# A hybrid scan and expert kernel on one core: a fuller plan for the experts beside the scans, and another order in the last stage

## The chip, the core and the metric

The kernel runs on one core of a Trainium2 chip. A core has a matrix engine (TensorE, PE in the profile; PEld are its weight loads), VectorE (DVE), ScalarE (ACT), GpSimd (POOL) and SyncE (SP), which here only issues DMAs. Each engine works through its own instructions in the order in which they stand; semaphores make it wait for others. The metric is the device time in microseconds, the median of the runs shown.

## What is computed

Two images of 256 channels and 4096 positions go through two layers. Layer 0 is a selective scan (a state-space model with 16 states per channel) with a residual. Layer 1 is a pair of such scans with 512 inner channels, one forward, one backward over the positions, with a residual, and then a mixture of eight small networks ("experts"):

```python
x = x + scan(group_norm(x))                       # layer 0, 256 inner channels
t = tokens(x)
n = layer_norm(layer_norm(t))
t = t + layer_norm(t) + scan_f(n) + flip(scan_b(flip(n)))   # layer 1, 512 inner channels each
n = layer_norm(t)
w = softmax(mean(n, over the two images) @ Wr + br)          # one weight per position and expert
h = relu(bn(n @ W1[e] + b1[e]))                              # for each of the 8 experts e
h = relu(bn(h @ W2[e] + b2[e]))
t = t + sum_e w[e] * (h @ Wo[e] + bo[e])
```

The routing weights `w` need both images. The experts' networks up to `h @ Wo[e]` need only one image's `n`, so they can run before `w` is known.

## The kernel before

Everything is float32. Positions are cut into 8 chunks of T = 512; a chunk of one image is held as two tiles of 128 channels. There are six scan jobs one after another: for each image layer 0, layer 1 forward, layer 1 backward. A job takes its 8 chunks in order.

**The scans and their slots.** The work beside the scans is laid out in slots: slot `2*g + h` is half `h` of quad `g`, and there are 640 quads, so 1280 slots. In each slot the emitting loop puts, in this order: DMA issues on SP, loads that have become due, TensorE's work (`pe`, then the sums over states `emit_sum`, then `pe2`), ScalarE's work (the carry, the next slot's decays L664, then `act`), VectorE's scan L690 and gates, the products with C (L699 on VectorE, L715 on GpSimd) and GpSimd's products L654. `sl.put(slot, queue, fn)` hangs any other work into a slot of a queue. The quads' buffer `bq` has six copies; TensorE's sums L723 free them.

**Features.** When a chunk of the backward job is done, `features` computes its layer-norm for the experts: mean on TensorE, centre on VectorE (L794), squares on ScalarE (`fsq`, L799), variance on TensorE (`fvar`, L804), root on ScalarE, division on VectorE (L809), and a store to DRAM (`nf_dram`, L814), each in a slot of its own, counted from the slot in which the chunk is stored. `ready` lists from which slot on the chunk may be used. The last chunk of image 1 has no slots left and gets its norm in the last stage.

**Experts beside the scans.** A pair is one expert on one chunk of one image; there are 2 x 8 x 8 = 128. A pair's three layers are 12 products of 128x512 (each layer: two output halves of two products). The planner `experts` walks over the slots and keeps two running sums: how many products TensorE is behind (a slot has room for `PE_ROOM` = 3.8 of them, and no half layer is added where more than `PE_BEHIND` would be behind) and the same for ScalarE. It also looks whether one of three PSUM banks is free. `follows` says from which slot a half layer may come: two slots after its input, and a number of slots after the last use of the weights' single buffer by the pair before (the `5` below; 6 for a chunk's first product), because `load_w` (L932) loads the weights three slots after that use. `emit_experts` then hangs the products (L912), activations (L923) and stores of the unweighted output `u` into their slots. Seventy-four pairs are placed so: all of image 0 (64), chunk 7 of image 1 (8) and two pairs of chunk 6.

**The last stage.** What the planner did not place runs after the scans, from L1062 on. `whole` are the chunks both of whose images are done (chunk 7), `rest` the others from the highest down (6, 5, ... 0). All experts' weights stay in SBUF; those not needed first are loaded in the first pairs (`weights`). For a chunk `i`, `load_n` (L1086, on GpSimd's DMA queue) brings both images' `n` into a tile with six buffers, `both` (L1108, GpSimd) adds them, `logits` (L1115) and `spread` (L1140 to 1146) make the routing weights and broadcast them through DRAM into `wb`, `bias` (L1163, L1166) adds the output biases, and `add_early` (L1170 to 1172) loads an early pair's `u`, multiplies it by its weight and adds it on VectorE. These steps are spread over the pairs of `rest` as `side` work. A pair computes two layers (L1201, L1205), `weigh` (L1212, VectorE) multiplies the hidden tile by the routing weight one pair later, and `last_layer` (L1220) multiplies by Wo another pair later. That is, the list `waiting` holds two pairs.

Of the kernel before, what the change touches and what calls it, by code (L numbers as in the profile page):

```python
# [42 lines left out]
F32 = mybir.dt.float32  # L43
# [4 lines left out]
P = 128  # L48
NB, C, L = 2, 256, 4096
KC = C // P  # L50
T = 512
# [28 lines left out]
E = 8  # L80


PE_ROOM, PE_BEHIND = 3.8, 2.5
ACT_ROOM, ACT_BEHIND = 2.6, 1.2
V_CW, V_CB, V_DB, V_D, V_A = 0, 4, 5, 6, 7
NV = V_A + NS
# [45 lines left out]
def hybrid_kernel(ctx: ExitStack, tc: tile.TileContext, a: dict, out: bass.AP):  # L132
# [45 lines left out]
    def rsqrt(dst, src, eps, scale=1.0):  # L178
        nc.scalar.activation(dst, src, AF.Ln, bias=eps, scale=scale)
        nc.scalar.activation(dst, dst, AF.Exp, scale=-0.5)  # L180
# [5 lines left out]
    with ExitStack() as st:  # L186
# [594 lines left out]
        def features(b, c, v, s0):  # L781

            featured.add((b, c))

            def mean():
                v["ps"] = psp.tile([P, T], F32, tag="ps", name=f"fmean_{b}{c}")
                for k in range(KC):
                    nc.tensor.matmul(
                        v["ps"], mean_w, v["x"][:, k, :], start=(k == 0), stop=(k == KC - 1)
                    )  # L790

            def centre():
                v["cen"] = wk.tile([P, KC, T], F32, tag="cen", name=f"fcen_{b}{c}")
                nc.vector.tensor_tensor(v["cen"], v["x"], over_channels(v["ps"]), ALU.subtract)  # L794

            def square():
                for k in range(KC):
                    v["sq", k] = wk.tile([P, T], F32, tag="th", name=f"fsq_{b}{c}{k}", bufs=3)
                    nc.scalar.activation(v["sq", k], v["cen"][:, k, :], AF.Square)  # L799

            def variance():
                v["var"] = psp.tile([P, T], F32, tag="ps", name=f"fvar_{b}{c}")
                for k in range(KC):
                    nc.tensor.matmul(  # L804
                        v["var"], mean_w, v["sq", k], start=(k == 0), stop=(k == KC - 1)
                    )

            def divide():
                nc.vector.tensor_tensor(v["cen"], v["cen"], over_channels(v["var"]), ALU.mult)  # L809

            for d, queue, fn in (
                (0, "pe", mean), (1, "dve", centre), (2, "act", square), (3, "pe", variance),
                (4, "act", lambda: rsqrt(v["var"], v["var"], eps5)), (5, "dve", divide),
                (6, "sp", lambda: nc.sync.dma_start(nf_dram[b][:, c, :, :], v["cen"])),  # L814
            ):
                sl.put(s0 + d, queue, fn)
            sl.count(s0, 2, 0, (1,))
            sl.count(s0 + 1, 0, 2)
            sl.count(s0 + 3, 2, 2, (2,))
            ready.append((s0 + 8, b, c))  # L820

        def scales():

# [23 lines left out]
        def experts():  # L847

            last = 2 * nq - 6
            banks = sorted(sl.banks, key=lambda r: r[0])  # L850

            def fits(slot):

                at = sum(b[0] <= slot for b in banks)
                both = banks[:at] + [(slot, slot + 1, 0)] + banks[at:]
                return all(
                    both[k - 3][1] + both[k][2] <= both[k][0] for k in range(max(3, at - 2), min(len(both), at + 4))
                    if at in range(k - 3, k + 1)
                )

            def sums_in(slot):
                n, h = divmod(slot % 16, 2)
                return 1.25 * len(SUMS.get((n, h), ())) + (1 if (n, h) in ((2, 0), (6, 0)) else 0)

            todo = [(at, b, c, e) for at, b, c in sorted(ready) for e in range(E)]
            behind = act_behind = 0.0
            times = [[], [], []]

            def follows(l):

                k, m = divmod(len(times[l]), KC)
                if k == len(todo):
                    return None
                waits = [(l - 1, k * KC + 1, 2)] if l else []
                if m:
                    waits.append((l, k * KC, 0))
                elif k:

                    waits.append((l, k * KC - 1, 6 if l == 0 and todo[k][-1] == 0 else 5))
                    if l < 2:  # L880
                        waits.append((l + 1, k * KC - 1, 0))
                if any(n >= len(times[w]) for w, n, _ in waits):
                    return None
                return max([todo[k][0] + 3] + [times[w][n] + d for w, n, d in waits])

            for slot in range(last):
                behind = max(0.0, behind) + sl.products.get(slot, 0) + sums_in(slot) - PE_ROOM
                act_behind = max(0.0, act_behind) + sl.acts.get(slot + 1, 0) - ACT_ROOM
                for l in (2, 1, 1, 0, 0):
                    at = follows(l)  # L890
                    if at is None or slot < at:
                        continue
                    if behind + 2 > PE_BEHIND or act_behind + 1.3 > ACT_BEHIND or not fits(slot):
                        break
                    banks.insert(sum(b[0] <= slot for b in banks), (slot, slot + 1, 0))
                    times[l].append(slot)
                    behind += 2
                    act_behind += 1 if l == 2 else 1.3
            put = [
                (*item[1:], [times[l][k * KC + m] for l in range(3) for m in range(KC)])  # L900
                for k, item in enumerate(todo) if (k + 1) * KC <= len(times[2])
            ]
            emit_experts(put)
# [158 lines left out]
    with ExitStack() as st:  # L1062
# [12 lines left out]
        for i in range(NCH - 1, -1, -1):  # L1075
            (whole if all(first[b, i] == E for b in range(NB)) else rest).append(i)

        def load_n(i):

            for b in range(NB):  # L1080
                n[b, i] = mk.tile([P, KC, T], F32, tag="n", name=f"n_{i}{b}", bufs=6)
                if (b, i) in featured:
                    src = nf_dram[b][:, i, :, :]
                else:
                    src = t_dram[b][:, :, i * T : (i + 1) * T]
                nc.gpsimd.dma_start(n[b, i], src)  # L1086
# [107 lines left out]
            nc.sync.dma_start(we[name, e], a[name][e].rearrange("(k p) n -> p k n", p=P))  # L1194

        def layer(x, l, e, tag):
            h = mk.tile([P, KC, T], F32, tag=f"h{l}", name=f"h{l}_{tag}", bufs=2 + l)
            for m in range(KC):
                ps = psp.tile([P, T], F32, tag="ps", name=f"hp{l}_{tag}_{m}")
                for k in range(KC):  # L1200
# [10 lines left out]
        def weigh(b, i, e, h):  # L1211
            nc.vector.tensor_tensor(h, h, over_channels(wb[i][:, e, :]), ALU.mult)  # L1212
# [39 lines left out]
        nc.sync.dma_start(bo, a["bo"])  # L1252
        layer_norm(rest[0])
        both(rest[0])
        weights = [("Wo", order[0])]
        for k in range(2, E):
            weights += [("W1", order[k]), ("W2", order[k]), ("Wo", order[k - 1])]
# [5 lines left out]
        for at, (b, i, e) in enumerate(pairs):  # L1263
# [6 lines left out]
                logits(i)  # L1270
            elif at == 1:
                spread(i)
            if waiting:
                weigh(*waiting[-1])
            waiting.append((b, i, e, h))
            if len(waiting) > 2:
                last_layer(*waiting.pop(0))
            done[i] += 1
            work = side[i] if at > 1 else []
# [111 lines left out]
```

## Time and profile before

The three runs took 5184.88 us in the median (5181.89 to 5185.45).

| what | value |
|---|---|
| the profiled execution's own time | 5183.55 us |
| its span on the core | 5181.8 us |
| mean granted TensorE clock | 0.917 |
| last product with the state sums (L723) | 4501.9 us |
| first product of the last stage (L1201) | 4527.3 us |
| pairs in the last stage | 54 |
| DMA over the span | 160 GB/s |

The page gives busy times over the whole span; since the kernel has a long stage with scans and a short one without, the stretches of the span are to be read one by one. A slot's pace can be read from VectorE's gates (L742), of which one falls on every eight slots: 54.5 us for sixteen slots in the steady parts.

### The profile page before, as it was taken

What the parts mean: (1) busy time and instruction counts of PE and PEld (TensorE: products, weight loads), DVE (VectorE), ACT (ScalarE), POOL (GpSimd) and SP (SyncE); (2) the same over time, 40 slices, a digit from 0 to 9 for tenths busy, and PEclk for the clock granted to TensorE, in tenths of its full rate; (3) what the DMA queues carried; (4) which work ended last, traced back from release to release, by engine and by line L of the source; (5) the groups of instructions that cost most, each with busy time, mean ns of one, the idle gap of its engine ahead of it and who ended that gap; (6) DMA issues with size and microseconds to landing.
All of it is one profiled execution on the core that took longest, in us unless ns stands there. A gap on an engine that the chain in (4) does not pass through costs nothing. (4 is left out here: it accounts for less than half of the span.)

```text
span 5181.8 us, 47299 instructions
## 1 busy us (share of the span) xinstructions
PE 4292.9 (83%) x14920; PEld 1483.9 (29%) x14920; DVE 4577.8 (88%) x3083; ACT 3681.3 (71%) x7462; POOL 4410.4 (85%) x1438
## 2 busy tenths in 40 slices
PE   5677677766668898888888888889899899689999
PEld 1222122222122233332222233223333333234444
DVE  6998999999999999999989999999999999746333
ACT  5778677777767888888887788888788888522332
POOL 5998999999999999999989999999999999611010
PEclk8888888887889999999999999999999999889999
DMA  4454433344334554555555544455544555354322
GB/s 176 154 178 163 154 127 139 129 152 154 135 131 160 195 185 164 182 171 196 191 185 177 191 159 174 155 181 191 178 165 165 173 183 175 117 189 155 111 104 77
DMA packets 314731, 834.47 MB, mean 161 GB/s; under 512 B 35240, under 2 KB 102064, under 8 KB 272496
## 3 DMA queue, kind: packets, MB, share of 16 engines
q1 hardware_dynamic: 310768, 806.15, 45.1%
q0 software_dynamic: 3712, 25.30, 1.3%
q8 instruction: 118, 1.93, 0.1%
q14 instruction: 133, 1.09, 0.1%
HBM read 647.18 MB, written 184.16 MB: 160 GB/s over the span
## 5 line engine op out<-in xcount | busy, mean ns | idle before, releaser
L654 POOL TENSOR_TENSOR bq<-rxdt,bc 128x2048 f32<-128x2048 f32 x640 | 2893.3, 4543 | 26.9 <-issue 11.8
L664 ACT ACTIVATE da<-rdt,w_a 128x512 f32<-128x512 f32 x2560 | 1756.5, 686 | 98.4 <-DVE bq L690 53.0
L690 DVE TENSOR_TENSOR_SCAN da<-da,h_state,bq 128x1024 f32<-128x1024 f32 x664 | 1559.2, 2348 | 63.8 <-ACT da L664 34.4
L715 POOL TENSOR_TENSOR bq<-bq,bc 128x2048 f32<-128x2048 f32 (+1 forms) x280 | 1180.0, 4214 | 22.5
L690 DVE TENSOR_TENSOR_SCAN bq<-da,h_state,bq 128x1024 f32<-128x1024 f32 x456 | 1058.6, 2338 | 20.3 <-ACT da L664 20.2
L723 PE MATMUL y<-bq,stack 128*32 128x512 f32 x5120 | 765.4, 691 | 347.4 <-POOL bq L715 324.1
L699 DVE TENSOR_TENSOR bq<-da,bc 128x1024 f32<-128x1024 f32 x760 | 926.5, 1219 | 15.9
L912 PE MATMUL e<-eh,ew 128*128 128x512 f32 x1184 | 578.6, 619 | 59.1 <-ACT eh L923 16.9
L709 ACT COPY h_state<-da 128x2 f32<-128x2 f32 x759 | 119.5, 157 | 680.0 <-DVE bq L699 678.5
L675 ACT ACTIVATE bq<-h_state,bq,a 128x1 f32<-128x1 f32 x1120 | 430.0, 384 | 0.7 <-POOL bq L654 0.2
L1205 ACT ACTIVATE h<-hp,of,sc 128x512 f32<-128x512 f32 x216 | 167.9, 778 | 347.4 <-PE hp L1201 330.3
L723 PEld LDWEIGHTS y<-bq,stack 128*32 128x32 f32 x5120 | 144.0, 118 | 906.1 <-POOL bq L715 461.1
L452 PE MATMUL conv<-xs,w_conv 64*64 64x512 f32 x2560 | 329.8, 604 | 24.4 <-ACT xs L436 21.4
L414 PE MATMUL z<-nx,w_in 128*128 128x512 f32 x640 | 324.7, 640 | 25.0 <-DVE sp L513 12.4
L414 PE MATMUL xs<-nx,w_in 128*128 128x512 f32 x640 | 317.5, 626 | 28.2 <-DVE xc L466 13.3
L912 PEld LDWEIGHTS e<-eh,ew 128*128 128x128 f32 x1184 | 214.2, 193 | 419.0 <-issue 209.0
L912 PE MATMUL e<-en,ew 128*128 128x512 f32 x592 | 286.1, 616 | 43.1 <-DVE sz L543 15.9
L761 PE MATMUL o<-sz,w_out 128*128 128x512 f32 x640 | 304.6, 616 | 0.0
L730 PE MATMUL y<-xc,w_d 128*128 128x512 f32 x320 | 193.6, 689 | 66.0 <-DVE sz L742 55.4
L517 POOL TENSOR_TENSOR xdt<-sp,xc 128x512 f32<-128x512 f32 x160 | 203.5, 1275 | 51.8 <-DVE sp L513 51.8
L923 ACT ACTIVATE eh<-e,of,sc 128x512 f32<-128x512 f32 x296 | 224.3, 770 | 30.5 <-PE e L912 29.9
L501 PE MATMUL dt<-dbc,w_dt 64*128 64x512 f32 x320 | 192.2, 695 | 41.2 <-ACT dbc L488 27.0
(138 smaller groups left out, 5045.5 us busy)
## 6 DMA issues: line engine op xcount, KB each, us to landing
rxdt<-xdtd SPq DMA_DIRECT2D x160, 1024.0 KB, 6.5
rdt<-dtd SPq DMA_DIRECT2D x160, 1024.0 KB, 6.3
bc<-bcd SPq DMA_DIRECT2D x384, 256.0 KB, 3.2
dtd<-sp SPq DMA_DIRECT2D x160, 256.0 KB, 3.6
xdtd<-xdt SPq DMA_DIRECT2D x160, 256.0 KB, 3.4
ew<-in_W SPq DMA_DIRECT2D x148, 256.0 KB, 4.9
u<-eu SPq DMA_DIRECT2D x74, 512.0 KB, 4.0
u<-u SPq DMA_DIRECT2D x74, 512.0 KB, 4.0
```

Source lines behind the costliest of these rows:

```text
L414: nc.tensor.matmul(ps, job.w["in", half][:, k, j * P : (j + 1) * P], rhs, start=(k == 0), stop=(k == KC - 1),)
L452: nc.tensor.matmul(v[r][64 * col : 64 * col + 64, :], job.w["conv"][rows, 2 * jp + j, k, :], ck["xs", jp][rows, j, k : k + T] if k < 4 els ...
L654: nc.gpsimd.tensor_tensor(bq[g], ck["rxdt", j], over_groups(ck["bc", 0, sg]), ALU.mult)
L664: nc.scalar.activation(da[g, h][:, k, :], cks[i]["rdt", j][:, q, :], AF.Exp, scale=steps[i][0].w["a"][:, j, q * SG + sg : q * SG + sg + 1],)
L675: nc.scalar.activation(bq[g][:, q, 0:1], job.h[:, j, sg, q : q + 1], AF.Identity, scale=cks[i]["a0", j][:, h, sg : sg + 1], bias=bq[g][:, ...
L690: nc.vector.tensor_tensor_scan(b if on_pool(g, h) else d, d, b, job.h[:, j, sg, 2 * h : 2 * h + 1] if c else 0.0, ALU.mult, ALU.add,)
L699: nc.vector.tensor_tensor(bq[g][:, two, :], d, cks[i]["bc", 1, sg].rearrange("p (o t) -> p o t", o=1).to_broadcast([P, 2, T]), ALU.mult,)
L715: nc.gpsimd.tensor_tensor(b, b, cks[i]["bc", 1, sg].rearrange("p (o t) -> p o t", o=1).to_broadcast([P, groups, T]), ALU.mult,)
L723: nc.tensor.matmul(y[i, j][q * CG : (q + 1) * CG, :], stack, bq[g][:, q, :], start=False, stop=(sg == SG - 1),)
L761: nc.tensor.matmul(v[m], job.w["out"][:, j, m * P : (m + 1) * P], ck["sz", j], start=False, stop=(j == job.nj - 1),)
L912: nc.tensor.matmul(ps, ew[l][:, k, m * P : (m + 1) * P], key[x][:, k, :], start=(k == 0), stop=(k == KC - 1),)
L923: nc.scalar.activation(key[dst][:, m, :], key["ps", l, m], AF.Relu, bias=of[:, l, e, m : m + 1], scale=sc[:, l, e, m : m + 1],)
```

## The change

There are six edits. The planner's limit `PE_BEHIND` goes from 2.5 to 3.0. In `features` the variance and all that follows come one slot later. The gap between the last use of an expert's weights and the next pair's first product goes from 5 to 4 slots. In the last stage `rest` is sorted so that a chunk with some of its pairs done comes after those with fewer done. The loads of `n` for the first chunk of `whole` and the second of `rest` are issued right after the first chunk's sum. The second hidden tile `h1` gets four buffers instead of three, `waiting` holds three pairs instead of two, and the weighting of the first three pairs is put behind the third and fourth pair's layers.

With the new numbers the planner places 83 pairs: all of image 0, chunks 7 and 6 of image 1, and three pairs of chunk 5. So `whole` is chunks 7 and 6, and `rest` is 4, 3, 2, 1, 0, 5.

```diff
-PE_ROOM, PE_BEHIND = 3.8, 2.5
+PE_ROOM, PE_BEHIND = 3.8, 3.0
...
-                (0, "pe", mean), (1, "dve", centre), (2, "act", square), (3, "pe", variance),
-                (4, "act", lambda: rsqrt(v["var"], v["var"], eps5)), (5, "dve", divide),
-                (6, "sp", lambda: nc.sync.dma_start(nf_dram[b][:, c, :, :], v["cen"])),
+                (0, "pe", mean), (1, "dve", centre), (2, "act", square), (4, "pe", variance),
+                (5, "act", lambda: rsqrt(v["var"], v["var"], eps5)), (6, "dve", divide),
+                (7, "sp", lambda: nc.sync.dma_start(nf_dram[b][:, c, :, :], v["cen"])),
             ):
                 sl.put(s0 + d, queue, fn)
             sl.count(s0, 2, 0, (1,))
             sl.count(s0 + 1, 0, 2)
-            sl.count(s0 + 3, 2, 2, (2,))
-            ready.append((s0 + 8, b, c))
+            sl.count(s0 + 4, 2, 2, (2,))
+            ready.append((s0 + 9, b, c))
...
-                    waits.append((l, k * KC - 1, 6 if l == 0 and todo[k][-1] == 0 else 5))
+                    waits.append((l, k * KC - 1, 6 if l == 0 and todo[k][-1] == 0 else 4))
...
+        rest.sort(key=lambda i: sum(first[b, i] for b in range(NB)))
+
         def load_n(i):
 
+            if (0, i) in n:
+                return
             for b in range(NB):
...
-            h = mk.tile([P, KC, T], F32, tag=f"h{l}", name=f"h{l}_{tag}", bufs=2 + l)
+            h = mk.tile([P, KC, T], F32, tag=f"h{l}", name=f"h{l}_{tag}", bufs=2 + 2 * l)
...
         layer_norm(rest[0])
         both(rest[0])
+        for i in whole[:1] + rest[1:2]:
+            load_n(i)
...
-            if waiting:
-                weigh(*waiting[-1])
+
+            for p in {0: [], 1: [], 2: waiting[:1], 3: waiting[1:]}.get(at, waiting[-1:]):
+                weigh(*p)
             waiting.append((b, i, e, h))
-            if len(waiting) > 2:
+            if len(waiting) > 3:
                 last_layer(*waiting.pop(0))
```

## The prediction

> **What bounds the kernel now.** I read the page's shares and slices first, then the busy time by stage, then who waits for whom, then TensorE's instructions in order of time where the last stage begins.
>
> ```profile
> PE 4292.9 (83%) x14920; PEld 1483.9 (29%) x14920; DVE 4577.8 (88%) x3083; ACT 3681.3 (71%) x7462; POOL 4410.4 (85%) x1438
> ...
> PE   5677677766668898888888888889899899689999
> ...
> DVE  6998999999999999999989999999999999746333
> ...
> POOL 5998999999999999999989999999999999611010
> ```
>
> The shares hide two stages. For 34 of 40 slices VectorE and GpSimd are full; after that GpSimd falls to a tenth and only TensorE is full. By stage (columns: length, then busy us and count on PE, weight loads, DVE, ACT, POOL, then granted clock, DMA share, GB/s):
>
> ```profile
> 3000.00:3500.00 500.00, 433.66 (x1607) 149.06 (x1607) 491.19 (x319) 408.79 (x847) 497.33 (x159) 0.95 0.49 169
> ...
> 4800.00:4900.00 100.00, 99.90 (x243) 43.16 (x242) 34.73 (x32) 29.97 (x40) 12.22 (x11) 1.00 0.37 133
> ```
>
> While the scans run, GpSimd works 497 of 500 us: it is the bound, with VectorE (491) next. In the last stage TensorE works 99.9 of 100 us. So a matrix product costs its full length in the last stage, and beside the scans only what it delays on GpSimd or VectorE. The waits beside the scans (total us, times, longest; the first line is 2800 to 4436 us, the others 1600 to 4500 us):
>
> ```profile
> POOL h_state L714 <- DVE bq L690: 6.5, 9, 1.7
> ...
> ACT h_state L709 <- DVE bq L699: 386.5, 347, 2.5
> ACT eh L923 <- PE e L912: 29.9, 41, 2.5
> ...
> PE fvar L804 <- ACT fsq L799: 43.5, 15, 4.2
> ```
>
> GpSimd's only wait in that stretch is 6.5 us, and not on TensorE. ScalarE waits 386 us for VectorE, so it runs ahead of it: that is its slack. It waits for an expert's product 30 us in all, and TensorE waits about 2.9 us in each of 15 features for the squares.
>
> TensorE's order of time where the last stage starts (start, length, instruction, idle time before it):
>
> ```profile
> 4527.28 6.52 PE L1201 MATMUL hp<-n,W 128*128 128x512 f32 x8 [13.73 <-DMA Wo<-in_Wo]
> ...
> 4560.39 5.35 PE L1220 MATMUL y<-h,Wo 128*128 128x512 f32 x8 [6.36 <-DVE h L1212]
> ...
> 4581.76 1.01 PE L1140 MATMUL wt<-ident,w 128*8 128x128 f32 x4 [1.65 <-DVE w L1134]
> ...
> 4602.40 3.58 PE L1115 MATMUL lt<-wr,nm 128*128 128x8 f32 x16 [6.57 <-POOL nm L1108]
> ...
> 4664.49 3.70 PE L1220 MATMUL y<-h,Wo 128*128 128x512 f32 x8 [3.58 <-DVE h L1212]
> ...
> 4679.34 5.40 PE L1220 MATMUL y<-h,Wo 128*128 128x512 f32 x8 [4.01 <-DVE h L1212]
> ...
> 5137.57 3.60 PE L1201 MATMUL hp<-n,W 128*128 128x512 f32 x8
> ...
> 5148.15 3.60 PE L1201 MATMUL hp<-n,W 128*128 128x512 f32 x8
> ```
>
> Five stalls after the start, 6.36 + 1.65 + 6.57 + 3.58 + 4.01 = 22.2 us, and behind them products run slow: eight that take 3.60 us in the steady part take 6.52 after the first wait and 5.35 and 5.40 after two others. The last two lines are two pairs' starts in the steady part: a pair costs 5148.15 - 5137.57 = 10.58 us.
>
> **What the skill says.** "TensorE: Matmul & The Clock Gate", section "What's actually happening": an idle window of about 3.4 us drops TensorE to half clock, and a busy one brings it back. The trace agrees: granted clock 0.50 in 4520 to 4530 us, and 6.52 for 3.60 us. "DMA: Bandwidth & Descriptors", section "Issuing engines are not separate DMA queues": loads issued from GpSimd and from SyncE share the same 16 DMA engines. The trace agrees: in 4530 to 4540 us, with both queues' loads under way, the DMA share is 1.08 at 356 GB/s. "Perfetto Trace Analysis", section "Identifying the Most-Contended Engine": occupancy ranks VectorE, ScalarE and GpSimd, but a busy TensorE is not one at its peak. So I take its cost from start-to-start times.
>
> **The change part by part.**
>
> (1) 83 instead of 74 pairs beside the scans. Working the planner's loop with the new numbers (room 3.0 behind, weights' gap 4, features 8 slots to 9) gives 83 pairs; the last product moves from slot 1267 to 1269 of 1280. The last stage keeps 128 - 83 = 45 pairs: 9 x 10.58 = 95.2 us off the stage where TensorE is the bound. The nine outputs come back as loads and additions on VectorE: 9 x (1.31 + 1.35) = 24 us, minus 9 x 1.22 for the weighting; VectorE works 35 of 100 us there, so TensorE hides it.
>
> What these nine cost beside the scans: 9 x 12 products of 0.88 us (10.58 / 12; the trace shows each as two records) = 95 us at full clock, 100 at 0.95, in a stretch where TensorE has room: from 1500 to 4500 us it is busy 2623. In the fullest even stretch, 4109 to 4218, it works 100.6 of 109 us; there a chunk gets two half layers (4 products, 3.7 us) more. That leaves about 5 us, before what part 2 frees. GpSimd needs TensorE's sums only when bq's buffers come round, six quads later. Chunks of the forward job pace the same with experts (3.476 and 3.344 us a slot by halves, mean 3.41) as without (3.524 and 3.329, mean 3.43), so I see no price per product yet. Floor: a gain of 8 us, if the rare waits go. Ceiling: 30 us, a third of the moved work. I take +4.
>
> (2) Variance, roots, division and store of a feature one slot later. This removes up to 15 x 2.9 = 43 us of TensorE waiting for squares. It lies beside GpSimd, so nothing is credited but cover for part 1. The store is one slot later on SP, and its reader waits for the slot given in `ready`, moved by one too.
>
> (3) The weights' gap 5 to 4. A load is issued three slots after the layer's last use, so a pair at the closest gap has one slot (3.4 us) less for it. At gap 5 the median time from issue to first product is now 11.5 us and the shortest 3.5, worked out by pairing the 222 loads of L932 with the products of L912; the load lands in 4.6 us (2.5 to 11.1). At gap 4 the median is then 8, still above. Of 36 such cases perhaps 6 wait 1 to 2 us each: up to 10 us on TensorE, behind which queue that slot's later products and the next slot's sums. It is inside the ceiling above.
>
> (4) Loads ahead. Four loads of 512 KB move behind the first sum on GpSimd's queue, past nothing but the routing weights' round trip, which starts 18 us later. They remove the 6.57 us wait for n and the slow products behind it (3.58 for 1.85 and 6.50 for 3.60). Price: 2 MB more beside 6 MB of weights, 2 / 0.35 = 6 us of saturated DMA before the broadcast weights' 2 MB. These now land at 4559; 0 to 3 us later are possible.
>
> (5) Three behind instead of two. The first last-layer product comes after four pairs' first two layers, with logits, weights' transposes and a bias between them: 4527.3 + 10.4 + 1.7 + 7.3 + 0.4 + 7.3 + 1.9 + 7.2 = 4563.5 by the lengths of the same instructions now, when the broadcast has landed and one weighting (1.2) is done or nearly. So 6.36 shrinks to between 0 and 3. The 3.58 and 4.01 us waits are VectorE late with a weighting behind additions; a further pair of slack (10.58 us) covers both. Two chunks now carry 24 additions (24 x 2.45 + 8 x 1.22 = 69 us of VectorE in 85 us of pairs); before one did. At four or five additions in a pair VectorE falls behind by 1 to 4 us a pair for four pairs, under the two pairs it has. No new stall.
>
> (6) Order of chunks, h1's fourth buffer: the partly done chunk last means 8 pairs for the first chunk instead of 6, over which the weights are spread. No instruction more. At the end the last four pairs' outputs follow one another instead of three, the same products.
>
> Slow products that go with the stalls, each against its steady length: 1.75 (5.35 for 3.60) + 2.5 (6.12 for 3.60) + 1.7 + 2.9 + 1.8 = 10.7 us. Stalls and these make 22.2 + 10.7 = 32.9; I leave 5 for the first wait and the start. Sum: -95.2 - 28 + 4 = -119. The profiled execution took 5183.55 us (span 5181.8 and 1.75 around it) and becomes 5064.5; the median of the runs is 1.3 above it, so 5066.
>
> **The rivals.** B, the stalls stay in another form: 2 MB more at the saturated start and 83 instead of 74 outputs (512 KB each) to load delay the broadcast weights or the additions. For it: in 4590 to 4600 the DMA share is 0.92 with TensorE idle. Against it: 0.6 at 200 GB/s through the additions' chunk. Then -95 - 5 + 4, about 5089.
>
> C, TensorE becomes the bound in parts of the scans: stretches around slots 984 to 1064, at up to 16 half layers beside 17 other products, come with the scans' own sums and skips (12) to 17 + 12 + 32 = 61 products in 16 slots, 61 x 0.88 / 0.95 = 56.5 us against 54.6 at the usual pace. If half of the moved work shows, +50: -95 - 28 + 50 gives 5112.
>
> D, slower: TensorE half a product (0.44 us) later in a slot keeps ScalarE waiting at the expert's activation, which stands in front of the next decays; VectorE's scan waits, and with 98% busy it never catches up. Price 0.44 us a slot, over 822 slots with experts; it decides from 123 / 0.44 = 280 slots on. If half of them lose it, 181 us: about 5243. Against it: ScalarE waits for expert products only 30 us now and has 386 us of waiting for VectorE to spend first.
>
> E, the planner places the pairs but VectorE's additions bound the last stage: 83 x 2.66 + 45 x 1.22 = 276 us in some 525. No. Nor can the plan fail to move the pairs: it is fixed arithmetic.
>
> **How the numbers follow.** A has 0.62, B 0.16, C 0.14, D and its like 0.07, no effect 0.01. A's own span is from all stalls gone and the scans 8 us shorter (-136, 5049) to half the stalls kept and 30 us lost in the scans (-80, 5104); B and most of C lie in it or just above. I take 5046 to 5106. About 0.2% (10 us) is what a measurement of this kernel can tell from no change. A, B and C are faster by far more: 0.92; within 0.01; slower 0.07.
>
> **What would show it.** Right: GpSimd still over 490 of 500 us until the scans end, at about 4515 us; the first last-stage product at 4525 to 4535; then 45 pairs 10.58 us apart, no idle of TensorE over 3 us, and about 525 us to the end. Part 2: the wait of fvar for fsq gone from TensorE. Part 3 wrong: expert products waiting for ew. C: slots of 3.5 us and GpSimd waiting for PE sums. D: ScalarE's wait for expert products in the hundreds of us and VectorE's for decays with it. The forecast fails if the scans end more than 30 us later.

## The result, and the profile after

The changed kernel took 5151.5 us in the median (5149.9 to 5153.9), the kernel before 5185.1 in the same comparison: a ratio of 0.9937, with a 95% interval from 0.9920 to 0.9954. It is faster by 0.6%, where 2.3% was forecast (5066 us), and outside the forecast range. The profiled execution took 5149.87 us, its span 5148.1.

Where the 120 us that were forecast went is read from two instants, the last state sum (L723) and the first product of the last stage (L1205 here, since the lines moved by four). This is TensorE's order of time in the changed kernel (start, length, instruction, idle time before it and its releaser):

```profile
4564.95 1.92 PE L723 MATMUL y<-bq,stack 128*32 128x512 f32 x4 [1.61 <-DVE bq L699]
...
4589.37 5.12 PE L1205 MATMUL hp<-n,W 128*128 128x512 f32 x8 [12.94 <-DMA Wo<-in_Wo]
...
4623.81 3.60 PE L1224 MATMUL y<-h,Wo 128*128 128x512 f32 x8
...
4753.54 3.58 PE L1119 MATMUL lt<-wr,nm 128*128 128x8 f32 x16 [11.69 <-POOL nm L1112]
4758.78 1.01 PE L1144 MATMUL wt<-ident,w 128*8 128x128 f32 x4 [1.65 <-DVE w L1138]
...
4785.93 0.60 PE L1144 MATMUL wt<-ident,w 128*8 128x128 f32 x4 [1.65 <-DVE w L1138]
...
4869.07 3.58 PE L1119 MATMUL lt<-wr,nm 128*128 128x8 f32 x16 [2.59 <-POOL nm L1112]
...
4879.94 3.70 PE L1205 MATMUL hp<-h,W 128*128 128x512 f32 x8 [2.22 <-ACT h L1209]
...
5131.62 3.70 PE L1224 MATMUL y<-h,Wo 128*128 128x512 f32 x8 [1.66 <-DVE h L1216]
...
5137.55 5.40 PE L1224 MATMUL y<-h,Wo 128*128 128x512 f32 x8 [2.23 <-DVE h L1216]
```

The scans end at 4564.95 us instead of 4501.9: 63 us later. From its first product to the end, the last stage takes 5148.1 - 4589.4 = 558.7 us instead of 654.5: 95.8 shorter. Together 33 us shorter, as measured. In the last stage the first product with Wo (4623.81) now waits for nothing, and the four other stalls of before are gone too. But seven other stalls, 23.7 us together, stand elsewhere, the longest 11.69 us for the next chunk's summed n. The 22.2 us have moved, and the stage got shorter by about what nine pairs take.

The scans, by stage (length, then busy us and count on PE, weight loads, DVE, ACT, POOL, then clock, DMA share, GB/s). First the second stretch in the kernel before, whose first one stands in the prediction:

```profile
3500.00:4000.00 500.00, 454.84 (x1681) 156.18 (x1679) 482.41 (x312) 401.44 (x830) 495.35 (x159) 0.96 0.51 177
```

Then both in the changed kernel:

```profile
3000.00:3500.00 500.00, 441.86 (x1642) 150.46 (x1641) 475.87 (x306) 398.98 (x825) 483.91 (x152) 0.96 0.49 168
3500.00:4000.00 500.00, 459.44 (x1620) 161.70 (x1619) 463.94 (x300) 401.44 (x818) 471.54 (x153) 0.96 0.53 179
```

GpSimd, 497 of 500 us busy before in the first stretch, is down to 484, and in the second from 495 to 472, with VectorE. TensorE has 8 us more in the first and 5 in the second. No engine is as full as GpSimd was. What GpSimd waits for, and VectorE (1600 to 4480 us; total us, times, longest), first in the kernel before:

```profile
POOL h_state L714 <- DVE bq L690: 39.8, 31, 5.0
...
DVE bq L690 <- ACT da L664: 20.8, 17, 2.2
```

and in the changed kernel:

```profile
POOL h_state L714 <- DVE bq L690: 102.7, 47, 5.1
...
DVE bq L690 <- ACT da L664: 65.9, 53, 2.3
...
DVE da L690 <- ACT da L664: 28.4, 34, 2.1
...
ACT h_state L709 <- DVE bq L699: 287.7, 279, 2.2
...
ACT eh L923 <- PE e L912: 41.0, 50, 1.9
```

GpSimd's wait for VectorE grew by 63 us, as much as the scans are late. It stands ahead of the quads (0, 2 and 5 of eight) whose products with C are GpSimd's work; these are also the quads whose scan writes `bq`. There VectorE does two scans with no product between them (2.34 us each), needs the decays of both halves in quick order, and waits 45 us more for them. ScalarE's own wait for VectorE, its slack, shrank from some 380 us to 288.

### The profile page after: what moved, and what is told of

Its sections match the earlier page's. It is cut to its first block, busy times and chain, and to the rows that moved or that the text cites. A ratio compares the mean times of both kernels' runs of the same rounds, so it can differ in the third digit from the quotient of the medians.

```text
span 5148.1 us, 47384 instructions
## 1 busy us (share of the span) xinstructions
PE 4290.5 (83%) x14920; PEld 1484.0 (29%) x14920; DVE 4588.7 (89%) x3091; ACT 3689.1 (72%) x7480; POOL 4409.0 (86%) x1438
## 4 chain that ended last, share of the span: by engine, by line
DVE 27%; PE 18%; ACT 13%; issue 5%; POOL 5%; DMA 3%; SPq 0%; DVEq 0%; POOLq 0%; ACTq 0%
DVE da L690 12%; ACT da L664 6%; DVE bq L699 6%; PE hp L1205 4%; DVE bq L690 4%; PE e L912 4%; POOL bq L654 3%; PE y L1224 2%; PE conv L452 2%; PE y L723 2%; PE o L761 1%; POOL bq L715 1%; ACT bq L675 1%; DVE x L1176 1%; DVE u L1175 1%
## 5 line engine op out<-in xcount | busy, mean ns | idle before, releaser
L654 POOL TENSOR_TENSOR bq<-rxdt,bc 128x2048 f32<-128x2048 f32 x640 | 2892.8, 4542 | 25.9 <-issue 14.4
L723 PE MATMUL y<-bq,stack 128*32 128x512 f32 x5120 | 767.0, 689 | 320.2 <-POOL bq L715 295.4
L699 DVE TENSOR_TENSOR bq<-da,bc 128x1024 f32<-128x1024 f32 x760 | 926.4, 1219 | 15.9
L912 PE MATMUL e<-eh,ew 128*128 128x512 f32 x1328 | 650.4, 619 | 78.7 <-DVE sp L513 18.1
L723 PEld LDWEIGHTS y<-bq,stack 128*32 128x32 f32 x5120 | 144.2, 119 | 889.0 <-POOL bq L715 399.5
L912 PEld LDWEIGHTS e<-eh,ew 128*128 128x128 f32 x1328 | 237.6, 192 | 483.4 <-issue 223.8
L912 PE MATMUL e<-en,ew 128*128 128x512 f32 x664 | 320.7, 613 | 20.5 <-DVE fcen L809 4.6
L1209 ACT ACTIVATE h<-hp,of,sc 128x512 f32<-128x512 f32 x180 | 139.9, 777 | 275.0 <-PE hp L1205 257.7
L923 ACT ACTIVATE eh<-e,of,sc 128x512 f32<-128x512 f32 x332 | 250.3, 769 | 42.0 <-PE e L912 41.0
L517 POOL TENSOR_TENSOR xdt<-sp,xc 128x512 f32<-128x512 f32 x160 | 203.2, 1272 | 51.8 <-DVE sp L513 51.7
L690 DVE TENSOR_TENSOR_SCAN da<-da,bq 128x1024 f32<-128x1024 f32 x96 | 219.5, 2287 | 6.2 <-ACT da L664 3.8
```

The costliest lines, as they stand in the source:

```text
L654: nc.gpsimd.tensor_tensor(bq[g], ck["rxdt", j], over_groups(ck["bc", 0, sg]), ALU.mult)
L690: nc.vector.tensor_tensor_scan(b if on_pool(g, h) else d, d, b, job.h[:, j, sg, 2 * h : 2 * h + 1] if c else 0.0, ALU.mult, ALU.add,)
L699: nc.vector.tensor_tensor(bq[g][:, two, :], d, cks[i]["bc", 1, sg].rearrange("p (o t) -> p o t", o=1).to_broadcast([P, 2, T]), ALU.mult,)
L723: nc.tensor.matmul(y[i, j][q * CG : (q + 1) * CG, :], stack, bq[g][:, q, :], start=False, stop=(sg == SG - 1),)
L912: nc.tensor.matmul(ps, ew[l][:, k, m * P : (m + 1) * P], key[x][:, k, :], start=(k == 0), stop=(k == KC - 1),)
L923: nc.scalar.activation(key[dst][:, m, :], key["ps", l, m], AF.Relu, bias=of[:, l, e, m : m + 1], scale=sc[:, l, e, m : m + 1],)
```

## The experiments

In each run, "scans' end" is the start of the last state sum in its profiled execution, against 4501.9 us before. Two runs whose time can't be told from that of before, those with the loads and with the later variance, have it 5.5 and 4.2 us later; so a few microseconds of it say nothing.

**The last stage alone.** The scans of before with its 74 pairs, and only the diff's edits from the last stage.

> The scans of before with its 74 pairs, and all edits of the last stage (order of chunks, loads ahead, three behind). The scans must end as before (first last-stage product at 4527 us). If the stalls at the start are removed and stay away, as the prediction had it, the last stage loses about 28 us: 5157. If they only move to later chunks, where the n of the next chunk is summed too late (11.7 us there in the changed kernel), the time falls by 0 to 12 us: 5173 to 5185.

It took 5160.5 us, ratio 0.9949 (0.9933 to 0.9966), and the scans' end moved by 2.5 us. So these edits do bring what the prediction gave them, 25.6 us of 28, as long as one chunk only is done beforehand: the rival of moved stalls is refuted for 74 pairs. What stalls remain come to 9.3 us, 2.4 of them (for the last chunk's norm) as before. In the changed kernel two chunks are done beforehand, and their additions stand in two stretches that follow each other.

**One suspected cost at a time, beside the scans.** In the kernel before, one half layer of every expert pair does part of its work twice (`nr` counts the pairs).

```diff
-                    for k in range(KC):
+                    for k in list(range(KC)) * (2 if (l, m) == (key["nr"] % 3, 0) else 1):
                         nc.tensor.matmul(
```

> Before, with one half layer of each of the 74 expert pairs beside the scans computed twice into the same PSUM tile: 148 more products on TensorE (74 x 1.83 us = 135 us at clock 0.95), and not one more activation, load or store. If TensorE's load is what the scans pay for, at the 1.15 us for a half layer by which the changed kernel's scans grew (62 us over 54 half layers), the scans end 74 x 1.15 = 85 us later: 5270. If the cost lies with ScalarE, the weights' loads or the stores, the time rises by less than 15 us.

5222.0 us, ratio 1.0072 (1.0057 to 1.0087); scans' end 40 us later. The 148 added products are 130 us of TensorE's work at 0.88 us; 40 of them show, about 0.5 us per half layer, between the two expectations.

The activation alone, or the copy where the layer is the third:

```diff
-                    if l == 2:
-                        nc.scalar.copy(key[dst][:, m, :], key["ps", l, m])
+                    for _ in range(2 if (l, m) == (key["nr"] % 3, 0) else 1):
+                        if l == 2:
+                            nc.scalar.copy(key[dst][:, m, :], key["ps", l, m])
...
```

> Before, with the activation of one half layer of each of the 74 pairs done twice: 74 x 0.77 = 57 us more on ScalarE, nothing on TensorE. If ScalarE's own work is the price, the scans end up to 57 us later: about 5240. If TensorE's load is, it costs under 15 us, since ScalarE waits 380 us for VectorE in this stretch.

5213.4 us, ratio 1.0053 (1.0038 to 1.0068); scans' end 28 us later. This lies between the two expectations: 50 activations of 0.77 us and 24 copies of 0.58 us, 52 us of added work, cost 28 on an engine that waited 380 us for VectorE.

Both edits together:

> Before, with one half layer of each of the 74 pairs computed twice and also activated twice: 148 products and 74 activations more, no loads and no stores more. The products alone cost 36 us and the activations alone 27. If both engines delay the scans one after the other, the two add up: 36 + 27 = 63, so 5249; then 54 half layers would cost 46 of the 62 us of the changed kernel, and 16 are left for the loads, the packing and the variance. If they hide behind one another, about 5225. If they make each other worse (each half layer 1.15 us as in the changed kernel), 74 x 1.15 = 85: 5271.

5233.3 us, ratio 1.0094 (1.0079 to 1.0109), scans' end 54 us later. They partly hide behind one another. Per half layer this is 49 / 74 = 0.66 us; at that rate the 54 half layers more of the changed kernel would cost 36 us, not 63.

**The loads, and the later variance.** First one of each pair's three weight loads also copied to a DRAM tile that nothing reads:

```diff
                 nc.sync.dma_start(ew[l], src)
+                if l == int(tag[-1]) % 3:
+                    spare = drp.tile([P, KC, C], F32, name=f"spare_{tag}")
+                    nc.sync.dma_start(spare, src)
```

> Before, with one of the three weights of each of the 74 pairs beside the scans also copied to a DRAM tile that nothing reads: 74 more DMA issues on SP of 256 KB each (18.9 MB; the changed kernel adds 27 of them and 9 stores of 512 KB, 11.5 MB). If SP's queue or the DMA engines are part of the price, the time rises by 10 us or more; if not, it stays within 3 us of before.

Ratio 1.0007 (0.9998 to 1.0016): nothing that can be told, and 8 us at most by the interval. Then the features' later slots alone, with the planner's counts left as they were:

```diff
-                (0, "pe", mean), (1, "dve", centre), (2, "act", square), (3, "pe", variance),
-                (4, "act", lambda: rsqrt(v["var"], v["var"], eps5)), (5, "dve", divide),
-                (6, "sp", lambda: nc.sync.dma_start(nf_dram[b][:, c, :, :], v["cen"])),
+                (0, "pe", mean), (1, "dve", centre), (2, "act", square), (4, "pe", variance),
+                (5, "act", lambda: rsqrt(v["var"], v["var"], eps5)), (6, "dve", divide),
+                (7, "sp", lambda: nc.sync.dma_start(nf_dram[b][:, c, :, :], v["cen"])),
```

> Before, with variance, roots, division and store of the features one slot later and the planner's counts and slots left as they were: the same 74 pairs in the same slots. If the later variance frees TensorE of its wait for the squares, as the prediction had it, the time is the same or up to 5 us less. If it stands behind another wait (for the PSUM bank of the time steps, 53 us on TensorE in the changed kernel), it costs up to 15 features x 1 us: 5186 to 5200.

Ratio 1.0005 (0.9996 to 1.0013): no price and no gain. TensorE's wait for the squares, 43.5 us before, got shorter all the same:

```profile
PE fvar L804 <- ACT fsq L799: 18.7, 11, 5.6
```

**The same number of pairs, packed as in the changed kernel.** Its planner stops after 74 pairs:

```diff
-                if k == len(todo):
+                if k == min(len(todo), 74):
```

> The changed kernel with its planner stopped after 74 pairs: the same denser packing (behind 3.0, gap 4, late variance) until they are placed, near slot 1180, then no experts beside the scans. Its last stage has the work of the run with the last stage's edits alone (654.5 less about 26 us). If the number of products beside the scans is what costs (a share per half layer, wherever it stands), the scans end within 8 us of before and the time is near 5160. If the denser packing costs (a fuller slot delays ScalarE and VectorE), the scans have lost some 55 us by slot 1180 and win back at most 2 us per 16 slots after it (about 13): the last stage starts some 40 us later and the time is near 5200.

5210.6 us, ratio 1.0048 (1.0033 to 1.0063); scans' end 50 us later, where the last stage's edits alone had 5160.5 with as many pairs. So most of the delay isn't the nine pairs: it is how the others are placed. It didn't win back what it had lost, either: 54 us were gone by slot 1160 and 57 by slot 1194, just after the last expert (slot 1192), and of these only some 7 came back.

**Which of the planner's numbers.** The changed kernel with one number of before each. First the limit:

```diff
-PE_ROOM, PE_BEHIND = 3.8, 3.0
+PE_ROOM, PE_BEHIND = 3.8, 2.5
```

> The changed kernel with the limit behind back at 2.5: 77 pairs beside the scans, 51 in the last stage. By the planner's own sums TensorE is then more than 2 products behind in 100 slots (103 before, 244 in the changed kernel). If that backlog is what delays the scans, they end 5 to 15 us later than before, and with the last stage of the run with its edits alone (5160 less 3 x 10.58) the time is near 5138. If the gap of 4 slots or the mere number of pairs costs (62 us over 9 pairs, or 20 us for 3, and more for the gap), the scans end 20 to 40 us later and the time is 5150 to 5168.

5147.2 us, ratio 0.9930 (0.9915 to 0.9945). The scans end where they did before (4502.0), with 77 pairs: at the old limit neither the gap of 4 nor three pairs more put them off. The time is 9 us over its expectation, through the last stage: a partly done chunk of only three pairs stands last, with 13 additions on VectorE, and TensorE waits:

```profile
5133.79 6.51 PE L1224 MATMUL y<-h,Wo 128*128 128x512 f32 x8 [16.32 <-DVE h L1216]
```

Then the weights' gap instead:

```diff
-                    waits.append((l, k * KC - 1, 6 if l == 0 and todo[k][-1] == 0 else 4))
+                    waits.append((l, k * KC - 1, 6 if l == 0 and todo[k][-1] == 0 else 5))
```

> The changed kernel with the weights' gap back at 5: 78 pairs, 50 in the last stage, and by the planner's sums more than 2 products behind in 219 slots. If the backlog is the cause, the scans end 40 to 55 us later than before and the time is near 5165. If the gap of 4 is, they end within 15 us of before and the time is near 5130.

5195.4 us, ratio 1.0023 (1.0013 to 1.0034); scans' end 47 us later. It ends slower than the kernel before, with four pairs fewer in its last stage; 24 us of stalls by the partly done chunk at the end are in it too. The limit is left, and one number changed in the kernel before shows it:

```diff
-PE_ROOM, PE_BEHIND = 3.8, 2.5
+PE_ROOM, PE_BEHIND = 3.8, 3.0
...
-                if k == len(todo):
+                if k == min(len(todo), 74):
```

> Before with one number changed, the limit behind from 2.5 to 3.0, and the planner stopped after the same 74 pairs; gap 5, features and last stage as before. If the limit (how much TensorE may be behind within a slot) is what delays the scans, they end 35 to 55 us later than before: 5220 to 5240. If the number of products is, or the gap of 4 with the limit, the time is within 12 us of before.

5231.0 us, ratio 1.0092 (1.0077 to 1.0107): the limit alone, with the same 74 pairs, delays the scans by 47 us. Its waits:

```profile
POOL h_state L714 <- DVE bq L690: 89.7, 40, 5.7
...
DVE bq L690 <- ACT da L664: 56.5, 48, 2.2
```

**Where in sixteen slots.** An activation of a product in slot p stands on ScalarE in slot p + 1, behind the decays of slot p + 2 and ahead of those of p + 3. For p = 2, 8 and 14 of sixteen those behind it are the second half's decays of a quad of GpSimd's. The limit of 2.5 leaves few half layers there, the limit of 3.0 twice as many. But a looser limit also lets TensorE be behind more often wherever it is. Both are counted here from the planner's slots; "behind" is the number of slots in which TensorE is more than two products behind by the planner's sums, at a room of 3.8 for all runs and rounded to tens:

| run | pairs | limit | half layers in slots 2, 8, 14 | behind | scans' end later | GpSimd waits for the scan, us |
|---|---|---|---|---|---|---|
| before | 74 | 2.5 | 42 | 100 | 0 | 39.8 |
| limit back at 2.5 | 77 | 2.5 | 41 | 100 | 0.1 | 47.3 |
| 79 pairs | 79 | 2.5 | 52 | 90 | 11 | 44.6 |
| the limit alone | 74 | 3.0 | 86 | 200 | 47 | 89.7 |
| gap back at 5 | 78 | 3.0 | 86 | 220 | 47 | 93.0 |
| stopped at 74 | 74 | 3.0 | 78 | 230 | 50 | 95.9 |
| changed kernel | 83 | 3.0 | 83 | 240 | 63 | 102.7 |
| 85 pairs | 85 | 2.5 | 57 | 200 | 59 | 88.2 |
| slots free | 74 | 3.0 | 0 | 140 | 15 | 51.8 |
| 80 pairs, slots free | 80 | 3.5 | 0 | 260 | 40 | 69.5 |

The run that tests the three slots is the kernel before with the limit at 3.0 and those three slots barred; 74 pairs come out of it:

```diff
-                    if at is None or slot < at:
+                    if at is None or slot < at or slot % 16 in (2, 8, 14):
                         continue
```

> Before with the limit at 3.0, as in the run with the limit alone (74 pairs, 5231), and the planner kept from slots 2, 8 and 14 of every sixteen; it still places 74 pairs. If the half layers in those slots are what delays the scans (44 more of them, 47 us), the delay goes: 5175 to 5195. If TensorE's being up to 3 products behind delays them wherever it happens, it stays: 5220 to 5235.

5196.1 us, ratio 1.0025 (1.0015 to 1.0036): 1 us over the upper end of what was expected. The scans end 15 us later and not 47:

```profile
POOL h_state L714 <- DVE bq L690: 51.8, 31, 5.0
...
DVE bq L690 <- ACT da L664: 14.4, 12, 2.2
```

VectorE's wait for the decays of those quads is 14.4 us, less than before the change. So 32 of the limit's 47 us go when the three slots are barred. That is not yet the price of those slots alone. Barring them also makes the plan looser elsewhere: it ends at slot 1267 instead of 1219, and of the 100 slots that the limit had added to those more than two products behind, 60 are gone as well. This run doesn't tell the two apart.

**More pairs at other limits.** All three have the gap of 4, the last stage's edits, and the features where the kernel before has them; the numbers are shown against the kernel before. The first has 79 pairs at the limit of 2.5, and the mixed additions that are shown further down:

> Features at their old slots, limit 2.5, gap 4 (79 pairs; by the planner's sums more than 2 products behind in 90 slots), the last stage's edits, and the finished chunk's additions mixed as in the run beside it. If the backlog theory holds, the scans end 5 to 15 us later than before, the last stage loses 5 x 10.58 + 26, and the time is near 5115, faster than both kernels. If the gap of 4 costs by itself, it is near 5140.

5161.0 us, ratio 0.9958 (0.9943 to 0.9972). The scans did what was expected (11 us later), the last stage didn't: a last chunk of a single pair carries 15 additions, and TensorE waits 39.5 us for its weighting.

The second lets TensorE have a little more of a slot, and has the partly done chunk second to last:

```diff
-PE_ROOM, PE_BEHIND = 3.8, 2.5
+PE_ROOM, PE_BEHIND = 3.9, 2.5
...
+        rest.insert(-1, rest.pop())
```

> The old limit of 2.5 and 85 pairs: the room of a slot at 3.9 instead of 3.8, gap 4, features at their old slots, the last stage's edits with the partly done chunk second to last. If only the limit costs, the scans end up to 25 us later than before. If it is the backlog however it comes about, they end about 45 us later, since the planner's sums at room 3.8 have 200 slots with more than 2 behind (103 before, 244 in the changed kernel). If it is the number of products, at 62 us for 9 pairs, 76 us later.

5140.4 us, ratio 0.9912 (0.9896 to 0.9929); scans' end 59 us later. That is over the 45 expected from the backlog and below the 76 from the number of pairs. Many pairs at the old limit are not free. The three slots don't explain it, with 57 half layers against 42 before. The slots more than two behind come nearer: they are as many as with the limit alone, which cost 47 us.

The third has a looser limit still and bars the three slots:

```diff
-PE_ROOM, PE_BEHIND = 3.8, 2.5
+PE_ROOM, PE_BEHIND = 3.9, 3.5
...
-                    if at is None or slot < at:
+                    if at is None or slot < at or slot % 16 in (2, 8, 14):
```

> 80 pairs (ten whole chunks, so no chunk is partly done) at a room of 3.9 and a limit of 3.5, with slots 2, 8 and 14 of sixteen kept free, features at their old slots, gap 4 and the last stage's edits. If those slots are the cause, the scans end 5 to 20 us later than before, and with 48 pairs in the last stage and the stalls of the changed kernel (558.7 + 3 x 10.58 = 590 us) the time is 5125 to 5140. If the limit is, the scans end 60 to 80 us later and the time is 5180 to 5200.

5156.3 us, ratio 0.9946 (0.9931 to 0.9961); scans' end 40 us later, between the two expectations. Here VectorE's wait is not at GpSimd's quads (13.3 us); ScalarE waits more for TensorE's products (63.9 us for `eh` against 29.9 before). The three slots are not the whole price. Nor is it the number of slots behind alone: 160 more than before would cost some 75 us at the rate of the limit alone (47 us for 100), by estimate.

**ScalarE's activations one slot later.** The changed kernel's products stay in their slots, and 239 of 502 activations move back by one, where reader and PSUM banks allow it:

```diff
-                        sl.put(slot + 1, "act", act)
+                        sl.put(slot + 1 + ((l, nr * KC + m) in late), "act", act)
```

> The changed kernel with the same 83 pairs in the same slots on TensorE, but 239 of the 502 activations of expert products one slot later on ScalarE, wherever their reader and the PSUM banks allow it. If ScalarE's waits for late expert products (59 us beside the scans), which stand in front of the next decays, are the link by which TensorE delays the scans, about half of the delay goes: the scans end 20 to 35 us earlier than in the changed kernel, 5118 to 5132. If TensorE's lateness acts by another way (banks, sums, the next chunk's projections), 5145 to 5160.

5160.4 us, ratio 0.9954 (0.9940 to 0.9969); the scans end 10 us later than in the changed kernel. The edit didn't remove the waits that it was aimed at: ScalarE waits 62 us for expert products, against 59 in the changed kernel. So whether they are the link stays untested. What it did move is the activations: by the planner's slots 43 are gone from ahead of those second decays and 53 have come there from the slot before each, 93 instead of 83. Yet VectorE's wait at GpSimd's quads fell from 65.9 us, and the one at the other quads rose from 28.4:

```profile
POOL h_state L714 <- DVE bq L690: 106.8, 54, 5.9
...
DVE da L690 <- ACT da L664: 46.6, 59, 1.8
DVE bq L690 <- ACT da L664: 39.9, 40, 2.2
```

So the number of activations in that place doesn't set VectorE's wait there, and with less of this wait the scans were not earlier.

**The last stage's new stalls.** Three tries on the changed kernel. Loads of x on GpSimd's queue instead of SP's:

```diff
-                nc.sync.dma_start(x[b, i], t_dram[b][:, :, i * T : (i + 1) * T])
+                nc.gpsimd.dma_start(x[b, i], t_dram[b][:, :, i * T : (i + 1) * T])
```

> The changed kernel with the last stage's loads of x issued on GpSimd's queue and not on SP's, where they stand behind loads of u that wait for their three buffers. If that is what keeps GpSimd waiting 52 us for x and the next n's sum behind it, TensorE's waits of 11.7 and 2.6 us for the sum go, and with them some 5 us of slow products: 5151 - 18 = 5133. If GpSimd is late for another reason, 5151 stays.

5165.1 us, ratio 0.9959 (0.9944 to 0.9974), no gain on the changed kernel. The wait for the sum of n there went, and its successor on VectorE became late:

```profile
4767.13 1.01 PE L1144 MATMUL wt<-ident,w 128*8 128x128 f32 x4 [14.46 <-DVE w L1138]
```

The additions of a finished chunk mixed with the routing steps:

```diff
-                    work += sums(j)
+                    now = sums(j) + now
```

> The changed kernel with the additions of a finished chunk mixed with the next chunks' routing steps and not all ahead of them; the scans are the same. If TensorE's waits of 11.7 and 2.6 us in the last stage come from routing steps that stand behind 16 additions on VectorE and GpSimd, they go and the time falls by 12 to 20 us, to about 5135. If the additions as such are too many, it stays at 5151.

5159.5 us, ratio 0.9951 (0.9934 to 0.9967). Again only the place changed: on ScalarE the softmax's exponential waits for VectorE's additions and holds up the next pair's activations behind it, for which TensorE waits in turn.

```profile
4865.95 0.23 ACT L1134 ACTIVATE w<-w 128x32 f32<-128x32 f32 x1 [26.18 <-DVE w L1133]
```

With the limit at 2.5 (77 pairs), the partly done chunk second to last:

```diff
         rest.sort(key=lambda i: sum(first[b, i] for b in range(NB)))
+        rest.insert(-1, rest.pop())
```

> The changed kernel with the limit at 2.5 (77 pairs) and the partly done chunk second to last instead of last. With it last, three pairs (32 us of TensorE) carry 13 additions (32 us of VectorE and their loads), and TensorE waits 16 us for the last weighting. If that is so, this wait goes: 5147 - 17 = 5130, faster than both kernels. If the additions are late for want of loads, it stays within 5 us of 5147.

5141.9 us, ratio 0.9921 (0.9906 to 0.9935). The wait of 16.3 us for the last weighting went, but 6.8 and 7.0 us of others came in the chunk before; the time lies between 5130 and 5147, and not apart from the run with the chunk last (0.9930) by its interval.

No run is safely below the changed kernel: the two lowest ratios, 0.9912 and 0.9921, have intervals that overlap with its own.

## Why the prediction was wrong

**The last stage's steady part was right.** Nine pairs at 10.58 us are 95.2 us, and the stage is 95.8 shorter. That the two agree so closely is chance: the stalls that went at its start and those that came later happen to weigh about the same. Its start was right too: the first product with Wo has no wait, and neither has the first next sum.

**Step 1 failed: "What these nine cost beside the scans", with a ceiling of 30 and +4 taken.** It measured 63. The prediction had read GpSimd's only wait, 6.5 us, from 2800 us on, where it is least; from 1600 us on it is the 39.8 above. The step reasoned from engine shares: TensorE has 109 - 100.6 us free, GpSimd's sums are due six quads later, ScalarE has 386 us to spend. Each of these is a sum over a stretch. What the step had no term for is how tightly the work is placed within it. It priced nine pairs, while the looser limit, which places the same 74 pairs differently, costs 47 us by itself, and 77 pairs at the old limit cost none. The delay shows as waits in between: VectorE's for the decays of GpSimd's quads grew from 20.8 to 65.9 us, and GpSimd's for VectorE with it. Keeping three slots free, in a plan that is then looser elsewhere too, takes 32 of the 47 us away. The forward job's pace with and without experts, which the step took as proof of no price, was that of the plan at the old limit, with half as many half layers in these slots and TensorE more than two products behind in 100 slots instead of 240.

**Steps 2 and 3 were right in their result.** Step 2 credited nothing for TensorE's wait for the squares, and the later variance alone took 25 us off it without any gain. As cover for the nine pairs it didn't serve: in the changed kernel another wait stands in its place, for VectorE's softplus, which by the program frees a PSUM bank.

```profile
PE fvar L804 <- DVE sp L513: 53.4, 11, 5.8
```

With the limit at 2.5 neither this (54.9 us there) nor the gap costs anything that can be told.

**Steps 4 and 5 were right by themselves** (25.6 us measured with 74 pairs, 28 taken), **and "No new stall" was wrong with 83.** Two finished chunks bring 24 additions into each of two following chunks. The step compared 69 us of VectorE with 85 us of pairs. It left out the loads. In the last stage up to 4880 us VectorE waited 10 us for GpSimd's bias, and 47.4 for the outputs `u`:

```profile
DVE u L1175 <- DMA u<-u: 47.4, 8, 13.2
```

It also left out that each of the two slows down beside the other: a multiplication of 1.22 us took

```profile
4748.05 3.25 DVE L1175 TENSOR_TENSOR u<-u,wb 128x1024 f32<-128x1024 f32 x1 [6.64 <-DMA u<-u]
```

while GpSimd added. The next chunk's sum on GpSimd stood behind a bias whose x was late by 52.5 us, as the x's load on SP's queue stood behind loads of u.

**The rivals.** B gave the last stage 100 us, its stalls kept (95.8 measured), and C gave the scans +50 (63 measured): both happened together. C's reason, TensorE as the bound, is not what the runs show for the larger part: 148 added products cost 40 us, but the products of the same 74 pairs, placed otherwise, cost 47 with none added, and GpSimd's wait for TensorE's sums, C's sign, went from 6.0 to 1.3 us. D's path (ScalarE's place ahead of the decays, then VectorE, then never caught up) is the nearer one, with 63 us where D would have had 181; but of its signs only VectorE's wait for decays came (45 to 94 us), while ScalarE's for expert products went from 40 to 59 us and not into the hundreds.

**What stays open.** How the tighter placing delays the scans: by half layers in those three slots, or by TensorE being behind in more slots of any kind. The run with the slots barred changes both. The one with 85 pairs is slow with few half layers there, the one with 80 is slow with none, and less so than its slots behind would have it. Nor is it known whether a half layer's product or its activation costs; the doubled products and activations show that both can. Of the last stage's stalls it is shown that they move when one load or the order is changed, not what would remove them.

## What to carry to other kernels

An engine at 90% beside two at 99% doesn't have 10% to give for certain: look at the single slots of the loop's period, at how far behind a new plan lets the engine be there, and at what waits behind it. When a planner's knob is loosened, hold the number of items fixed once and change the knob alone: here the packing, not the count, was the larger price. And stalls that are removed from the start of a stage should be looked for at its next boundary, behind the same in-order queue.

## What the runs showed that was not expected

A second activation or copy of 0.77 or 0.58 us, on an engine that waited 380 us of 2880 for another, put off the scans' end by 0.38 us each (28 us for 74). In the last stage VectorE's 1024-element multiplication took 3.25 us instead of 1.22 beside GpSimd's additions, whose own sum took 3.31 instead of 2.34. And taking the experts away after slot 1192 gave back only about 7 us of 57: from VectorE's gate at slot 1194 to its last the scans took 285.0 us, and 291.6 with the plan of before, which has experts there.
